# A relational graph layer with a gate: GpSimd's order written out, and two pieces of TensorE's order moved

## The chip, the cores and the metric

The kernel runs on one core of a Trainium2 chip. A core has five engines, each with an instruction queue of its own: TensorE (PE, the matrix products), VectorE (DVE), ScalarE (ACT), GpSimd (POOL) and SyncE (SP, which here only issues DMA transfers). The metric is the device time of one execution in microseconds. The time of a kernel is the median over its runs.

## The reference

A graph of 1250 nodes with 1024 features each, and 20,000 edges of eight relations:

```
x (1250, 1024) f32;  src, dst (20000,) int32, sorted by dst;  edge_type_8 (20000,) in 0..7
weight (8, 1024, 1024), root (1024, 1024), w_gate (2048, 1024), bias, b_gate (1024,)

h   = maximum(layernorm(x), 0)
u   = h @ root + bias
for r in 0..7:                                    # mean over the edges of relation r into a node
    mask = (edge_type_8 == r)
    sums = segment_sum(h[src] * mask[:, None], dst);  cnt = segment_sum(mask, dst)
    u   += (sums / maximum(cnt, 1)[:, None]) @ weight[r]
z   = concatenate([u, h], 1) @ w_gate + b_gate
out = x + tanh(u) * z + h * (1 - z)
```

## The kernel before

**Products.** Since the mean is linear, the kernel multiplies first and gathers afterwards: y_r = h @ weight[r] for all nodes, then u[node] is a weighted sum of rows of y. With `root` and the two halves of `w_gate` there are 11 products of 1280 x 1024 by 1024 x 1024, taken in the order weight[0..7], root (result `hr_dram`), the lower half of w_gate (for h; result `z_dram`), and last the upper half (for u). The nodes are ten blocks of 128 rows. They are worked in five pairs: blocks i and i+5, in the last product 2i and 2i+1. One pair times one matrix is a Strassen-Winograd product (`product`, L192): seven block products instead of eight, each four f32 matmuls of depth 128 onto 128 x 512. A f32 matmul leaves two records in the trace, so a block product has eight of line L201. Products 1 and 2 go to fresh PSUM banks b and c, 3 adds into b, 4 into c, 5 into b, 6 goes to a third bank, 7 adds into b. Between them ScalarE copies a bank out (L210 after the first, L213 after the second, L216 after the third, L223, L231 later) and VectorE adds others (L219, L224, L228). A product that adds into a bank waits for the copy of the bank's last state. The operands on the left (A11, A12, S1 to S4 of `h_op[i]`) come from transposes on TensorE (`transposed`, L177, copied out by ScalarE and VectorE) and four subtractions (`left`, L186 to L190). Those on the right, T1 to T4 (L157, L161, L165, L169), are made by VectorE once for each matrix.

**What sets the order.** `manual_schedule` names the engines that issue in the order of the program's text: PE, DVE, Activation and SP. GpSimd isn't among them: the scheduler chooses its order. After each block product `product` calls `between(j)`, j = 0 to 6; I call these seven places slots. All work beside the products is dealt out there, written as generators that are advanced one `yield` in a slot, so that a `yield` more puts what follows one slot later. In the first products `index()` runs there: `norms()` (layer norm, transposes and operands of pairs 1 to 4) side by side with `columns()`, then `slots()` and `order()`, which sort the edges into a table of slots per node. Pairs 0 and 1 are normed ahead of everything (`both(*b0)`, `both(*b1)`), and pair 1's transposes come in slot 4 of the first product. `both` gives VectorE the statistics and ScalarE the square root and the ReLU (L400, one 128 x 1024 instruction for a block). `with_x` (VectorE) makes x + h, which SP stores as `xh_dram`; `load_x` on SP brings later blocks of x, into buffers of which there are three.

**Edges.** Relations 0 to 2, 3 to 5 and 6 to 7 form three groups. In a group the nodes stand sorted by their count. `rows_and_weights(g)` writes that order to DRAM (ten scatters, L334), loads it back (`node`, L343), makes `node_key` (L344) and gathers the table rows (`idx`, L298), all by GpSimd. `edges(g)` then takes block by block: GpSimd gathers one row of y for each node (L823, into one of four buffers `got`), and VectorE adds it, weighted, to `u` (L829 for the first of group 0, L831 otherwise). A finished block of u is scattered to `u_dram` (`to_rows`, L303), from which the next group gathers it again (L298). Group 0's edges stand beside matrices 4 and 5, group 1's beside 6 and 7, group 2's beside 8 and 9. Group 0's carries along the preparation of groups 1 and 2 (`with_others`: one step of it after every second gather). `spread` deals the steps of a generator evenly over the slots. Ahead of group 1's edges `passes_needed` checks whether any node has more edges than slots: 28 reductions (L897, `far_k`), two small transposes of `most` on TensorE (L901, L902), and a count `n_pass` that all engines read, for a branch that this data doesn't take.

**Gate.** In the last product each pair needs rows that GpSimd gathers in node order: z and xh (`gate_rows`, L1049), hr, added to u by VectorE (`gate_load`, L1024, and behind it the transposes and operands of `gate_u`), and h. `finish` (L1122, L1123) joins them, and GpSimd scatters the rows of `out` (L303). In the text z and xh of a pair stand ahead of hr of the pair two on.

**Dependencies.** The scatters into one buffer write different rows. `declare_no_dep` with a group name tells the framework that they need not wait for each other.

Of the kernel before, what the change touches and what calls it, by code (L numbers as in the profile page):

```python
# [19 lines left out]
def tile_rgcn_highway(  # L20
# [29 lines left out]

    nc = tc.nc
    eng = mybir.EngineType
    ctx.enter_context(tc.manual_schedule(engines={eng.PE, eng.DVE, eng.Activation, eng.SP}))
    P = 128
    N, D = x.shape
    R = weight.shape[0]
# [21 lines left out]

    A11, A12, A22, S1, S2, S3, S4 = range(7)
    A21 = S3  # L80

    def nrows(d):
        return min(P, N - d * P)
# [207 lines left out]
    ids = const.tile([P, ND], I32, name="ids")  # L291
    pos_i = const.tile([P, G, ND], I32, name="pos_i")
    n_pass = const.tile([1, 1], I32, name="n_pass")
    h_op = [keep.tile([P, 7, KQ, P], F32, name=f"h_op{i}") for i in range(NP)]

    def rows_of(to, of, at):
# [3 lines left out]
            in_offset=bass.IndirectOffsetOnAxis(ap=at, axis=0))  # L300

    def to_rows(of, frm, at, group):
        ins = nc.gpsimd.indirect_dma_start(  # L303
            out=of, out_offset=bass.IndirectOffsetOnAxis(ap=at, axis=0), in_=frm, in_offset=None)
        tc.declare_no_dep(ins.ins, group=group, reason="rows differ")
        tc.add_to_no_dep_group(group, ins.ins)

    def slot_rows(g, of, to):
# [22 lines left out]
    def rows_and_weights(g):  # L331

        for d in range(ND):
            ins = nc.gpsimd.indirect_dma_start(  # L334
                out=node_dram[g][:, :],
                out_offset=bass.IndirectOffsetOnAxis(ap=pos_i[:, g, d:d + 1], axis=0),
                in_=ids[:, d:d + 1], in_offset=None,
                bounds_check=KEYS - 1, oob_is_err=False)
            tc.declare_no_dep(ins.ins, group="nodes", reason="places differ")
            tc.add_to_no_dep_group("nodes", ins.ins)  # L340
            if d % 2:
                yield
        nc.gpsimd.dma_start(node[:, g, :], node_dram[g].rearrange("(d p) o -> p (d o)", p=P))  # L343
        nc.gpsimd.tensor_single_scalar(node_key[:, g, :], node[:, g, :], g * KEYS, op=OP.add)  # L344
        yield
        yield
        for d in range(ND):
            rows_of(idx[:, g, d, :], table_rows, node_key[:, g, d:d + 1])
            if d % 2:
                yield  # L350

    with ExitStack() as early:
# [111 lines left out]
        fac[0].make_t3()  # L464
        left(h_op[0], 3)
        b1 = [Normed(1 + part * NP, x1[part], scratch(NP - 1 - part, 2)) for part in range(2)]
        both(*b1)
        fac[0].make_t4()
        for b in b0 + b1:
            b.store()  # L470
        for b in b0:
            b.with_x()
        xs += [load_x(2, 1), load_x(3, 0)]


        tb_col = ix1.tile([P, NCH], F32, name="tb_col")
# [74 lines left out]
        def slots(ix):  # L551
# [78 lines left out]
            def place(j):  # L630
                cs, o = chunks(j), now.pop(j)
                m, c0 = len(cs), cs[0]
                c1 = c0 + m
                p = psum.tile([P, 512], F32, name="ps_q", bufs=1)
                for i in range(m):
                    nc.tensor.matmul(p[:, i * 2 * NHI:(i + 1) * 2 * NHI], o["to_lo"][:, i, :],
                                     o["s_b"][:, i].rearrange("p a b -> p (a b)"),
                                     start=True, stop=True)
                q = p[:, :CG * 2 * NHI].rearrange("p (c a b) -> p c a b", a=2, b=NHI)
                own = ix.tile([P, CG, 2, NHI], F32, name="own", bufs=1)  # L640
                nc.vector.tensor_tensor(
                    own[:, :m], q[:, :m],
                    o["is_at"][:, :m, None, :NHI].to_broadcast([P, m, 2, NHI]), op=OP.mult)
                o2 = ix.tile([P, CG], F32, name="o2")
                nc.vector.reduce_sum(o2[:, :m], own[:, :m].rearrange("p c a b -> p c (a b)"),
                                     axis=AX.X)

                for i, c in enumerate(cs):
                    junk = ix.tile([P, P], F32, name="junk", bufs=1)
                    nc.vector.scalar_tensor_tensor(junk, o["k_bc"][:, i, :], key_col[:, c:c + 1],  # L650
                                                   before, op0=OP.is_equal, op1=OP.mult,
                                                   accum_out=rank[:, c:c + 1])
                nc.vector.tensor_add(rank[:, c0:c1], rank[:, c0:c1], o2[:, :m])
                over = ix.tile([P, CG], F32, name="over")
                nc.vector.tensor_single_scalar(over[:, :m], rank[:, c0:c1], float(SLOTS),
                                               op=OP.is_ge)
                at = ix.tile([P, CG], F32, name="at")
                nc.vector.tensor_add(at[:, :m], first[:, c0:c1], rank[:, c0:c1])
                at_i = ix.tile([P, CG], I32, name="at_i")
                nc.vector.scalar_tensor_tensor(at_i[:, :m], over[:, :m], float(FAR), at[:, :m],  # L660
                                               op0=OP.mult, op1=OP.add)
                for i, c in enumerate(cs):
                    n = nedges(c)
                    ins = nc.gpsimd.indirect_dma_start(  # L664
                        out=table[:, :],
                        out_offset=bass.IndirectOffsetOnAxis(ap=at_i[:n, i:i + 1], axis=0),
                        in_=row_col[:n, c:c + 1], in_offset=None,
                        bounds_check=G * KEYS * WIDE - 1, oob_is_err=False)
                    tc.declare_no_dep(ins.ins, group="scatter", reason="each edge has its own slot")
                    tc.add_to_no_dep_group("scatter", ins.ins)  # L670

            for j in range(ng + 3):
# [8 lines left out]
        def order():  # L681

            with tc.tile_pool(name="sort", bufs=1) as sp:
# [18 lines left out]
                for g in range(G):  # L702
                    ins = nc.sync.dma_start(
                        table[g * KEYS * WIDE:(g + 1) * KEYS * WIDE]
                        .rearrange("(d p s) o -> p d (s o)", p=P, s=WIDE)[:, :, SLOTS:],
                        rc.bitcast(I32))
                    tc.declare_no_dep(ins.ins, group="scatter", reason="beside the slots")
                one = sp.tile([P, 1], F32, name="one")
                nc.vector.memset(one, 1.0)
                for _ in range(4):  # L710
# [22 lines left out]
                    yield  # L733

        def norms():
            for _ in range(4):
                yield
            factored(1, b1)
            left(h_op[1])
            yield  # L740
            for b in b1:
                b.with_x()
            yield
            for i in range(2, NP):
                blocks = []
                if i < NP - 1:
                    blocks = [Normed(i + part * NP, xs.pop(0), scratch(NP - 1, part))
                              for part in range(2)]
                    both(*blocks)
                    yield  # L750
                    for b in blocks:
                        b.store()
                    yield
                    factored(i, blocks)
                    left(h_op[i])
                    yield
                    for b in blocks:
                        b.with_x()
                    xs.append(load_x(i + 1, 1))
                    if i + 2 < NP:  # L760
                        xs.append(load_x(i + 2, 0))
                    yield
                else:
                    for part in range(2):
                        xt = xs.pop(0)
                        b = Normed(i + part * NP, xt, xpool.tile([P, D], F32, name="xt"))
                        b.stats(0)
                        b.stats(1)
                        b.spread()
                        b.scale()  # L770
                        b.relu()
                        b.store()
                        yield
                        transposed(h_op[i], part, b.ht, b.n)
                        b.with_x()
                        yield
                    left(h_op[i])
            first_part.close()
# [19 lines left out]
    with ExitStack() as edges_part:  # L798
# [91 lines left out]
        def passes_needed():  # L890
# [3 lines left out]
            for g in range(G):  # L894
                for d in range(ND):
                    if K[g][d] < SLOTS:
                        nc.vector.reduce_max(far_k[:, g * ND + d:g * ND + d + 1],  # L897
                                             w_of[:, g, d, K[g][d]:], axis=AX.X)
            nc.vector.reduce_max(most[:, 1:2], far_k, axis=AX.X)
            p = bank()  # L900
            nc.tensor.transpose(p[:1, :P], most[:, 0:1], ident)  # L901
            nc.tensor.transpose(p[:1, P:2 * P], most[:, 1:2], ident)  # L902
# [32 lines left out]
        def with_others(e):  # L935
# [6 lines left out]
            for _ in others:  # L942
# [2 lines left out]
        weights(0)  # L945
        s, i = beside(with_others(edges(0, range(ND), u_back(0))), sum(K[0]) + 1, s, i,
                      R0[2] - 1)
        for g in range(1, G - 1):
            if g == G - 2:
                passes_needed()  # L950
            s, i = beside(edges(g, range(ND), u_back(g)), sum(K[g]) + 1, s, i, R0[g + 2] - 1)


        passes = nc.values_load(n_pass[0:1, 0:1], min_val=0, max_val=E // MORE,
# [216 lines left out]
```

## Time and profile before

| | |
|---|---|
| time, median of 3 runs | 1405.44 us (1404.57 to 1406.19) |
| profiled execution: its own time | 1409.36 us |
| its span, first to last instruction | 1407.5 us |
| its granted TensorE clock, mean | 0.991 of full |
| GpSimd's software DMA queue | 48,864 packets, 128.60 MB, 28.3% of the 16 DMA engines |
| SP's and ACT's hardware queues | 101.38 MB, 24.7%; 41.95 MB, 9.1% |
| HBM | 214.20 MB read, 80.65 MB written, 209 GB/s over the span |

The page cuts the span into 40 equal slices; each digit is a busy share, or the granted clock, in tenths:

```profile
PE   5999999999999999899999999999999999999996
...
PEclk8999999999999999999999999999999999999998
```

A row of the timeline has the start in us from the span's start, the length, the engine (a `q` behind it means its queue of DMA issues), the line in the kernel, the operation, output `<-` inputs with shapes, and how many instructions the row joins. In brackets stands how long the engine was idle before it, and what it waited for. A row of the waits has the waiting engine, its tile and line, the releasing engine with tile and line, then total us, how often, and the longest. "DMA node<-node_dram" names a transfer by its destination and source.

### The profile page before, as it was taken

The numbers are of one execution on the slowest core, as the hardware profiler recorded it, in microseconds if no ns is written. First come the engines' busy times: TensorE is split into PE (matmuls) and PEld (weight loads), VectorE is DVE, ScalarE is ACT, GpSimd is POOL, SyncE is SP. The second block draws the span as 40 slices with busy tenths as digits, with TensorE's granted clock in tenths as the row PEclk, the third lists the DMA queues.
The fourth block names the chain that finished last, engine by engine and source line by source line (L and its number), as shares of the span: only waits on it lengthen the run. The fifth ranks groups of instructions, "written<-read, shape, count | busy, mean of one in ns | idle before, by whom it ended". The sixth has DMA issues, their size and how long they took to land.

```text
span 1407.5 us, 11960 instructions
## 1 busy us (share of the span) xinstructions
PE 1369.5 (97%) x3562; PEld 617.6 (44%) x3562; DVE 862.2 (61%) x1658; ACT 339.0 (24%) x721; POOL 624.3 (44%) x537
## 2 busy tenths in 40 slices
PE   5999999999999999899999999999999999999996
PEld 2544444444444444344444444444444444444442
DVE  6764976886768723277454654645445564467983
ACT  3235656566521111011111011111111111122210
POOL 0001655565552657675344443445435433325531
PEclk8999999999999999999999999999999999999998
DMA  8554765775545234458776745888768654557751
GB/s 319 221 185 120 146 156 135 154 160 138 100 109 176 64 107 148 129 203 301 273 252 208 282 146 173 297 300 281 240 241 313 228 163 161 179 187 254 269 174 57
DMA packets 109863, 272.73 MB, mean 194 GB/s; under 512 B 25890, under 2 KB 27920, under 8 KB 109664
## 3 DMA queue, kind: packets, MB, share of 16 engines
q0 software_dynamic: 48864, 128.60, 28.3%
q1 hardware_dynamic: 39808, 101.38, 24.7%
q10 hardware_dynamic: 21120, 41.95, 9.1%
q8 instruction: 28, 0.46, 0.2%
q14 instruction: 43, 0.35, 0.1%
HBM read 214.20 MB, written 80.65 MB: 209 GB/s over the span
## 4 chain that ended last, share of the span: by engine, by line
PE 52%; issue 3%; DVE 2%; DMA 1%; POOL 1%; POOLq 0%; ACT 0%; DVEq 0%; ACTq 0%
PE ps L201 51%; DMA got<-y,idx 0%; PE ps L177 0%; DMA y<-row 0%; POOL out_dram L303 0%; DVE row L1122 0%; DVE u L831 0%; DVE w L1060 0%; DVE u L1024 0%; DVE w L1077 0%; DVE w L165 0%; DVE far_k L897 0%; DVE row L1123 0%; POOL got L298 0%; DVE row L228 0%
## 5 line engine op out<-in xcount | busy, mean ns | idle before, releaser
L201 PE MATMUL ps<-w,h_op 128*128 128x512 f32 x3080 | 1348.6, 597 | 14.3 <-ACT row L210 8.5
L201 PEld LDWEIGHTS ps<-w,h_op 128*128 128x128 f32 x3080 | 581.0, 191 | 711.9 <-issue 692.2
L823 POOL DMA_INDIRECT got<-y,idx x202 | 254.2, 1258 | 272.7 <-DVE u L831 215.6
L831 DVE SCALAR_TENSOR_TENSOR u<-got,w_of,u 128x1024 f32<-128x1024 f32 (+1 forms) x192 | 245.9, 1282 | 138.5 <-DMA got<-y,idx 135.9
L664 POOL DMA_INDIRECT table<-row_col,at_i x157 | 175.7, 1119 | 159.8 <-DVE at_i L660 71.0
L219 DVE TENSOR_TENSOR row<-row,ps 128x512 f32<-128x512 f32 x55 | 37.8, 686 | 158.9 <-PE ps L201 112.4
L223 ACT COPY part<-ps 128x512 f32<-128x512 f32 x55 | 32.1, 585 | 273.3 <-PE ps L201 273.3
L231 ACT COPY row<-ps 128x512 f32<-128x512 f32 x50 | 29.2, 585 | 258.8 <-PE ps L201 253.1
L224 DVE TENSOR_TENSOR row<-row,part 128x512 f32<-128x512 f32 x55 | 38.0, 690 | 61.4 <-ACT part L223 61.3
L210 ACT COPY row<-ps 128x512 f32<-128x512 f32 x55 | 32.1, 583 | 175.6 <-PE ps L201 162.1
L216 ACT COPY row<-ps 128x512 f32<-128x512 f32 x55 | 32.1, 583 | 139.9 <-PE ps L201 139.9
L213 ACT COPY row<-ps 128x512 f32<-128x512 f32 x55 | 32.1, 583 | 130.5 <-PE ps L201 124.6
L650 DVE SCALAR_TENSOR_TENSOR junk<-k_bc,key_col,before 128x128 f32<-128x128 int32 x157 | 55.0, 350 | 4.2
L334 POOL DMA_INDIRECT node_dram<-ids,pos_i x30 | 36.5, 1215 | 39.1 <-issue 38.8
L590 DVE TENSOR_TENSOR seen<-seen,ps_n 128x110 f32<-128x110 f32 x157 | 42.2, 269 | 15.5 <-PE ps_n L585 11.5
L228 DVE TENSOR_TENSOR row<-row,ps 128x512 f32<-128x512 f32 x55 | 37.6, 683 | 21.1 <-PE ps L201 21.1
L567 ACT ACTIVATE is_lo<-io,less_lo 128x128 bf16<-128x128 f32 x157 | 50.1, 391 | 0.8 <-DVE row L224 0.8
L157 DVE TENSOR_TENSOR w<-w,w 128x2048 f32<-128x2048 f32 x11 | 25.2, 2291 | 40.4 <-PE ps L201 39.9
L303 POOL DMA_INDIRECT u_dram<-u,node x20 | 25.2, 1261 | 54.4 <-DVE u L831 40.4
L718 DVE SCALAR_TENSOR_TENSOR junk<-v_bc,val,one 128x1280 bf16<-128x1280 f32 x30 | 46.5, 1550 | 4.0 <-DMA v_bc<-val_dram 3.3
L298 POOL DMA_INDIRECT idx<-table,node_key x30 | 35.8, 1195 | 9.2 <-issue 6.1
L298 POOL DMA_INDIRECT u<-u_dram,node x20 | 20.3, 1015 | 39.4 <-DMA last_dram<-u 14.3
(158 smaller groups left out, 715.3 us busy)
## 6 DMA issues: line engine op xcount, KB each, us to landing
y<-row SPq DMA_DIRECT2D x72, 512.0 KB
w<-in_L_gnn_weight_dram ACTq DMA_DIRECT2D x28, 1024.0 KB
k_bc<-keys_dram SPq DMA_DIRECT2D x39, 256.0 KB
l_bc<-los_dram SPq DMA_DIRECT2D x39, 256.0 KB
w<-in_L_gnn_w_gate_dram ACTq DMA_DIRECT2D x8, 1024.0 KB
hr_dram<-row SPq DMA_DIRECT2D x9, 512.0 KB
z_dram<-row SPq DMA_DIRECT2D x9, 512.0 KB
w<-in_L_gnn_weight_dram SPq DMA_DIRECT2D x4, 1024.0 KB
```

The costliest lines, as they stand in the source:

```text
L201: nc.tensor.matmul(b, aop[:, i, k, :], w.of[i][:, k, :], start=(fresh and k == 0), stop=(k == KQ - 1), skip_group_check=True)
L219: nc.vector.tensor_add(c12, c12, c)
L224: nc.vector.tensor_add(c22, c22, d)
L228: nc.vector.tensor_add(c11, c11, a)
L298: nc.gpsimd.indirect_dma_start(out=to, out_offset=None, in_=of, in_offset=bass.IndirectOffsetOnAxis(ap=at, axis=0))
L567: nc.scalar.activation(is_lo[:, i, :], io, AF.Abs, bias=less_lo[:, c0 + i:c0 + i + 1])
L590: nc.vector.tensor_add(seen[j][:, i, :], was, p[:, i, :])
L650: nc.vector.scalar_tensor_tensor(junk, o["k_bc"][:, i, :], key_col[:, c:c + 1], before, op0=OP.is_equal, op1=OP.mult, accum_out=rank[:, c: ...
L664: ins = nc.gpsimd.indirect_dma_start(out=table[:, :], out_offset=bass.IndirectOffsetOnAxis(ap=at_i[:n, i:i + 1], axis=0), in_=row_col[:n, ...
L718: nc.vector.scalar_tensor_tensor(junk, v_bc[:, g, :], val[:, c:c + 1], one.to_broadcast([P, KEYS]), op0=OP.is_gt, op1=OP.mult, accum_out=p ...
L823: nc.gpsimd.indirect_dma_start(out=t[:n], out_offset=None, in_=y[g][:, :], in_offset=bass.IndirectOffsetOnAxis(ap=at[:n, d, k:k + 1], axis=0),
L831: nc.vector.scalar_tensor_tensor(u[:n], t[:n], w, u[:n], op0=OP.mult, op1=OP.add)
```

## The change

1. GpSimd (`Pool`) joins the engines that issue in the order of the text. The tile `apart` is new: GpSimd clears it (128 x 1) ahead of every scatter of `to_rows`. `declare_no_dep` gets the argument `query=no_wait`, ANY_SYNC, in all four places: the scatters of `to_rows`, of `node_dram` and of the edges into the table, and the store beside the slots.
2. The second pair's norm: `both(*b1)`, `make_t4()` and the stores of h leave the text ahead of the first product, for slot 2, behind its third block product. Pair 1's transposes keep slot 4. `with_x` of pair 0, and the loads of x for the third pair's second block and the fourth pair's first, go to slot 5, `with_x` of pair 1 to slot 6, and one more `yield` puts all later pairs' norms two slots later.
3. `passes_needed` becomes a generator with three `yield`s between the reductions and the transposes. It is advanced once with each step of group 1's edges (`with_passes`).

```diff
-    ctx.enter_context(tc.manual_schedule(engines={eng.PE, eng.DVE, eng.Activation, eng.SP}))
+    ctx.enter_context(tc.manual_schedule(
+        engines={eng.PE, eng.DVE, eng.Activation, eng.Pool, eng.SP}))
...
+    no_wait = mybir.DependencyQuery.ANY_SYNC
...
+    apart = const.tile([P, 1], F32, name="apart")
...
     def to_rows(of, frm, at, group):
+        nc.gpsimd.memset(apart, 0.0)
         ins = nc.gpsimd.indirect_dma_start(
             out=of, out_offset=bass.IndirectOffsetOnAxis(ap=at, axis=0), in_=frm, in_offset=None)
-        tc.declare_no_dep(ins.ins, group=group, reason="rows differ")
+        tc.declare_no_dep(ins.ins, query=no_wait, group=group, reason="rows differ")
...
         b1 = [Normed(1 + part * NP, x1[part], scratch(NP - 1 - part, 2)) for part in range(2)]
-        both(*b1)
-        fac[0].make_t4()
-        for b in b0 + b1:
+        for b in b0:
             b.store()
-        for b in b0:
-            b.with_x()
-        xs += [load_x(2, 1), load_x(3, 0)]
...
         def norms():
-            for _ in range(4):
-                yield
+            yield
+            yield
+            both(*b1)
+            fac[0].make_t4()
+            for b in b1:
+                b.store()
+            yield
+            yield
             factored(1, b1)
             left(h_op[1])
             yield
+            for b in b0:
+                b.with_x()
+            xs.extend([load_x(2, 1), load_x(3, 0)])
+            yield
             for b in b1:
                 b.with_x()
+            yield
             yield
...
             nc.vector.reduce_max(most[:, 1:2], far_k, axis=AX.X)
+            for _ in range(3):
+                yield
             p = bank()
             nc.tensor.transpose(p[:1, :P], most[:, 0:1], ident)
...
+        def with_passes(e):
+            passes = passes_needed()
+            for _ in e:
+                next(passes, None)
+                yield
+
         for g in range(1, G - 1):
-            if g == G - 2:
-                passes_needed()
-            s, i = beside(edges(g, range(ND), u_back(g)), sum(K[g]) + 1, s, i, R0[g + 2] - 1)
+            e = edges(g, range(ND), u_back(g))
+            s, i = beside(with_passes(e) if g == G - 2 else e, sum(K[g]) + 1, s, i, R0[g + 2] - 1)
```

More of the change, by code (lines that the diff above doesn't have):

```diff
@@ L338, in rows_and_weights @@
                 bounds_check=KEYS - 1, oob_is_err=False)
-            tc.declare_no_dep(ins.ins, group="nodes", reason="places differ")
+            tc.declare_no_dep(ins.ins, query=no_wait, group="nodes", reason="places differ")
             tc.add_to_no_dep_group("nodes", ins.ins)
@@ L668, in place @@
                         bounds_check=G * KEYS * WIDE - 1, oob_is_err=False)
-                    tc.declare_no_dep(ins.ins, group="scatter", reason="each edge has its own slot")
+                    tc.declare_no_dep(ins.ins, query=no_wait, group="scatter", reason="each edge has its own slot")
                     tc.add_to_no_dep_group("scatter", ins.ins)
@@ L706, in order @@
                         rc.bitcast(I32))
-                    tc.declare_no_dep(ins.ins, group="scatter", reason="beside the slots")
+                    tc.declare_no_dep(ins.ins, query=no_wait, group="scatter", reason="beside the slots")
                 one = sp.tile([P, 1], F32, name="one")
```

## Prediction

> **What bounds the kernel now.** I read the busy shares first, then the waits of TensorE, then the timeline around each wait, since every product of the text stands in one TensorE queue.
>
> ```profile
> PE 1369.5 (97%) x3562; PEld 617.6 (44%) x3562; DVE 862.2 (61%) x1658; ACT 339.0 (24%) x721; POOL 624.3 (44%) x537
> ...
> PE ps L201 <- ACT row L210: 8.5, 2, 8.2
> ...
> PE ps L177 <- ACT h_op L400: 7.8, 2, 7.6
> ...
> PE ps L201 <- DVE row L228: 5.8, 1, 5.8
> ...
> PE ps L902 <- DVE most L899: 2.1, 1, 2.1
> ```
>
> TensorE bounds it: 97% busy, and what it waits for is a short list (columns: total, times, longest). In quiet stretches 56 L201 records take 24.05 us (the chain of work), so one record is 0.429 us; a block product has eight, so a slot is 3.43 us. The time can only move by what stands around these records: the start (7.6), three waits (8.2, 5.8, 2.1), the slow matmuls after each, new waits, and the tail. The waits answer to the change's parts. The windows of L201 alone show what follows a wait (columns: stretch; length, busy and records; granted clock; DMA share; GB/s):
>
> ```profile
> 27.32:40.72 13.40, 13.40 (x24) 0.77 0.93 339
> 559.78:584.40 24.62, 24.62 (x58) 1.00 0.12 16
> ```
>
> After the first wait 24 records took 13.40 us where 24 x 0.429 = 10.30 would do: 3.1 us more, at a clock of 0.77. After the second, 8 records took 5.17 for 3.43: 1.7 more. After the third, 35 took 16.88 for 15.03: 1.85 more.
>
> **Part 1, the second pair's norm behind the third product.**
>
> ```profile
> 25.56 1.24 ACT L400 ACTIVATE h_op<-h_op,less,rs 128x1024 f32<-128x1024 f32 x1 [0.42 <-DVE less L393]
> 26.71 0.56 ACT L210 COPY row<-ps 128x512 f32<-128x512 f32 x1
> ...
> 27.32 13.56 PE L201 MATMUL ps<-w,h_op 128*128 128x512 f32 x24 [8.16 <-ACT row L210]
> ```
>
> Products 1 and 2 end at 19.16. Product 3 adds into product 1's bank and waits for ScalarE's copy L210, which stands behind the norm of pair 1 (the last L400 ends at 26.80). In the new order L210, L213 and L216 stand ahead of that norm, so product 3 starts at 19.2: its factor T2 is made by 18.0 (L161 from 15.73, 2.28), its operand S2 by 15.8 (L187). Saved: 8.16 + 3.1 = 11.3 us. What is late next: the transposes of pair 1, in TensorE's queue behind product 5, now at 29.4. The norm starts after L216 (23.2) instead of at 22.9, so its last L400 ends near 27.3: 2 us in hand. VectorE's order there is unchanged but for `with_x` and the loads behind it. Those go from 27.6 to about 35.5 (two adds of 1.2), so the SP queue asks for x(2,1) near 39.6 (a store 2.85 later than the add, as 28.89 to 31.74 now); I estimate arrival at 44 to 45.6, 4 to 6 us for 0.5 MB at the 339 GB/s of that stretch. Pair 2's norm starts at slot 8 (45 to 46), takes 5.5 (49.08 to 54.54 now), and its transposes come at 51.9: 0 to 1.3 us in hand, and L216 of that product behind the norm. I take 0.5 us lost, between 0 and 3. Index work starts two slots later and has over 30 us in hand: group 0's last idx gather is issued at 490.03, and weights(0) runs at 530.16.
>
> **Part 2, GpSimd in the order of the text, group 0's gathers.**
>
> ```profile
> 536.02 1.03 POOL L334 DMA_INDIRECT node_dram<-ids,pos_i  x1 [0.30 <-issue]
> ...
> 564.71 1.02 POOL L343 DMA_DIRECT2D node<-node_dram  x1 [5.28 <-DMA node_dram<-ids,pos_i]
> ...
> 581.52 1.02 POOL L823 DMA_INDIRECT got<-y,idx  x1 [0.30 <-issue]
> ...
> 585.93 1.28 DVE L831 SCALAR_TENSOR_TENSOR u<-got,w_of,u 128x1024 f32<-128x1024 f32 x1 [30.62 <-DMA got<-y,idx]
> ```
>
> Now groups 1 and 2's node scatters, loads and idx gathers stand ahead of the fifth row gather; VectorE waits 30.6 us for it with TensorE's row adds queued behind, and TensorE 5.77. The built order puts group 0's gathers right after its own idx gathers (about 497, as two slots later) and deals the other groups out two DMAs per two gathers. So the wait goes: 5.77 + 1.7 + 0.34 (the next L210) = 7.8 us. In its place: group 1's `node` load holds GpSimd for 5.3 (scatters landing) + 2.4 to 6.8 (the load) at most, with up to four gathers out, four slots or 13.7 us of VectorE's work; and VectorE may be some 25 us late (30.6 less 5.8) before TensorE notices. I cost it at nothing; uncovered it would be those 5.8 again. A u scatter now stands behind two row gathers of the next block instead of three: also within that cover. The 30 small memsets `apart` are 0.1 us each (the 128x1 memsets at the start), on an engine busy 44%.
>
> **Part 3, the transposes three slots on.** The first step of edges(1) gathers, and VectorE's order becomes: T4, one L831, far_k's 28 reductions, three L831.
>
> ```profile
> 781.09 2.18 DVE L897 TENSOR_REDUCE far_k<-w_of 128x1 f32<-128x10 f32 x28
> ...
> 793.79 1.28 DVE L831 SCALAR_TENSOR_TENSOR u<-got,w_of,u 128x1024 f32<-128x1024 f32 x1 [6.54 <-DMA got<-y,idx]
> ```
>
> That L831 is group 1's first: it waits for u_dram's last scatter (781.32), the u gather (786.82) and the row gather (788.44), and cannot come sooner. So the reductions end at 793.79 + 1.28 + 2.2 + 0.2 = 797.5. And 76 steps over 70 slots put two steps into slot 0, so "three on" is slot 2: TensorE reaches the transposes after three products, 781.2 + 10.3 = 791.5. It waits 6.0 us where it waited 2.1. With 1.8 for the clock on both sides: 3.9 us lost (bounds 2 and 5.2, the latter with 3.1 for the clock).
>
> **Part 4, GpSimd in order at the gate.** Built order now: xh, xh, hr, hr, z, z. After: z, xh, z, xh, hr, hr.
>
> ```profile
> 1278.84 0.95 POOL L298 DMA_INDIRECT got<-hr_dram,node  x1 [0.30 <-DMA z_dram<-row]
> ...
> 1274.41 1.47 SPq L274 DMA_DIRECT2D z_dram<-row  x2
> ...
> 1286.38 1.23 DVE L1024 TENSOR_TENSOR u<-u,got 128x1024 f32<-128x1024 f32 x1 [8.66 <-DMA got<-hr_dram,node]
> 1288.78 1.23 DVE L1024 TENSOR_TENSOR u<-u,got 128x1024 f32<-128x1024 f32 x1 [1.18 <-DMA got<-hr_dram,node]
> ...
> 1291.91 0.69 DVE L186 TENSOR_TENSOR h_op<-h_op 128x512 f32<-128x512 f32 x1
> ```
>
> The first z gather waits for the last z store, issued by 1275.9 and landed near 1280.6 (a y store took 4.80 in the chain). Behind it stand xh, z, xh, each 1.25 apart, then hr at 1285.7 instead of 1278.84: 6.9 us later. VectorE's L1024 waits for hr, and behind it in its queue L186, ending at 1292.6, which becomes 1299.5. TensorE needs it after product 1 of the next pair, 1297.15 (ScalarE's L210 there starts at 1297.19). Wait: 2.4 us, plus 1.8 of clock = 4.2. The pair after has 3.5 us in hand (L186 done at 1319.4, needed at 1322.95) and a lag of 6.9 - 4.2 = 2.7: no wait. Bounds: 0 (the later hr stays inside the 4.5 us in hand: 1297.15 less 1292.6) and 10 (VectorE has 25.5 of 26 us busy from 1294 to 1320, so a lag is not worked off). After 1359 VectorE is idle again, so the tail keeps.
>
> **Two rules against rows.** (a) After the 2.1 us wait at 783.55 the clock fell (1.85 us). The Trainium skill, "TensorE: Matmul & The Clock Gate", What's actually happening, halves the clock only after an idle window of about 3.4 us: the gate's 2.4 would then cost 2.4, not 4.2. The row decides. (b) The hr gather at 1278.84 was used 7.5 us later. "DMA: Bandwidth & Descriptors", Anatomy of one DMA, fits 2.0 us + bytes/436e3, 3.2 us for these 512 KB: by an estimate from it the second hr (issued 1287.0 to 1287.9) is in at 1291.1, a lag of 2.4, inside the 4.5 in hand, and part 4 is free. I take the row, with the queue it includes, and keep 0 as the end.
>
> **Sum.** -11.3 + 0.5 - 7.8 + 3.9 + 4.2 = -10.5 us. The profiled execution took 1409.36, its span 1407.5 with 1.86 around it: the new span is 1397.0. The median is 3.9 below the profiled time: 1405.4 - 10.5 = 1394.9. With rule (a) alone 1393.1, with (b) 1390.7.
>
> **Rivals.** (R1) The gate absorbs the later hr: 1390.7. For it: the 4.5 us in hand; against: six gathers in a row. (R2) The lag shows again: 3 us in the second gate pair and 2 to 3 at pair 2's transposes: 1399 to 1402. For it: VectorE's full stretch. (R3) Slower: the gate's in-order queue. Without part 4 the change gives 14.7, so it is slower than noise from a gate cost of 17.5 up, which needs a lag of 4.5 + 15.7 = 20 us, hr issued at 1299 instead of 1285.7; three turns in which h, out and z gathers each hold the next hr by another 6.9 would do it. Against: hr of later pairs is issued 10 us before its use (1300.79, 1313.0). Price about 1410. (R4) It does nothing: the early wait comes back whole at the transposes of pairs 1 and 2, and parts 2 and 4 cancel: 1405.
>
> **How the numbers follow.** A measurement here tells 0.2%, 2.8 us, from nothing. Chances: the forecast 0.55 (its own range 1391 to 1399), R1 0.20, R2 0.12, R3 0.08, R4 0.05. Faster is the forecast, R1 and three quarters of R2: 0.84. Same is the rest of R2 and R4: 0.08. Slower is R3: 0.08. The range 1388.5 to 1402.5 leaves out R3, R4 and a little at the low end; its ends are parts 1 to 3 with nothing lost at pair 2 or the gate and part 3 at its lower bound (1388.3), and R2.
>
> **What would show it.** Right: no L201 wait on L210 near 19 us; no VectorE wait over 15 us near 530 to 590; a wait of about 6 us of the second `most` transpose; a z gather ahead of hr and a wait of about 2 us before the second product after it. Wrong: a TensorE wait at pair 1's or 2's transposes above 3 us, a wait on row adds in edges(0) or edges(1), or out scatters later against TensorE's end than now.

## The result: no change that counts, where 10 us were forecast

The changed kernel takes 1408.42 us (median of 17 runs, 1403.71 to 1410.70), the kernel before 1406.23 us (17 runs beside it): ratio 1.0017, 95% interval 1.0006 to 1.0028. That lies outside the forecast range (1388.5 to 1402.5), within 0.2% of the time before.

The profiled execution of the changed kernel took 1409.14 us, its span is 1407.3. TensorE's waits in it (columns: total, times, longest):

```profile
PE ps L915 <- DVE most L910: 14.4, 1, 14.4
PE ps L180 <- ACT h_op L405: 10.9, 3, 7.6
PE ps L204 <- DVE h_op L189: 2.9, 2, 2.8
PE ps L180 <- ACT xt L405: 2.2, 2, 1.4
```

Two of the old waits, 8.2 and 5.8 us, are gone. The one at the small transposes grew from 2.1 to 14.4, and three are new or longer (7.6 of L405 is the start, as before).

**A ledger of TensorE's lead.** ScalarE copies `part` (L223 before, L226 after) behind the fifth block product of each of the 55 pairs. The start of the n-th such copy, less its start in the trace of before, says how far TensorE is ahead (negative) or behind at that place. Where the difference jumps, time was won or lost. For the changed kernel:

| place | lead, us | step | forecast |
|---|---|---|---|
| first pair of the first matrix | -11.7 | first wait gone: -11.7 | -11.3 |
| first pair of the second matrix | -5.5 | other pairs' norms: +6.1 | +0.5 |
| matrix 4, pair 1, then pair 2 | -5.6, -13.7 | group 0's gathers: -8.1 | -7.8 |
| matrix 6, first pair | -1.0 | small transposes: +12.7 | +3.9 |
| last matrix, first pair, then second | -1.0, +5.5 | gate: +6.5 | +4.2 |
| behind the last scatter | -0.2 | end of program: -5.7 | 0 |

So the two profiled executions differ by 0.2 us. The medians differ by 2.2 the other way, because the profiled execution of before is 3.1 us over its own median, that of after 0.7. One term that varies is the old wait in group 0's edges: 5.8 us in that trace, between 0.9 and 6.1 in traces of kernels below that leave GpSimd's order and TensorE's start alone.

**Where the early gain went back.** Timeline of the changed kernel, the fourth pair (index 3):

```profile
64.39 1.57 SPq L369 DMA_DIRECT2D xt<-in_x_dram  x2
...
68.57 0.69 DVE L388 BATCH_NORM_STATS2 st<-xt 128x6 f32<-128x512 f32 x1 [3.75 <-DMA xt<-in_x_dram]
...
69.60 1.24 ACT L405 ACTIVATE h_op<-xt,less,rs 128x1024 f32<-128x1024 f32 x1 [4.39 <-DVE less L398]
...
70.90 1.09 PE L180 MATMUL ps<-ident,h_op 128*128 128x128 f32 x8 [2.50 <-ACT h_op L405]
```

Its second x block gets a buffer only when pair 2's `with_x` is stored. It is loaded at 64.4, and VectorE, ScalarE and TensorE wait for it in turn: 2.50 us and 0.81 at pair 3, 0.79 and 1.45 at pair 4, 5.6 in all, where TensorE had waited 1.1 before. Behind the first of these waits the granted clock was 0.72 over 6 us, which cost about 1.7 more: 6.1 together. In norm_only below the same text waits 4.4 us, the clock stays at 1.00, and 3.3 us go. Pair 2, the one that I had checked, waits for nothing.

**At the small transposes.** The changed kernel, the end of group 0's edges and the start of group 1's:

```profile
764.35 1.03 POOL L308 DMA_INDIRECT u_dram<-u,node  x1 [6.81 <-DVE u L842]
765.69 2.07 POOL L834 DMA_INDIRECT got<-y,idx  x1 [0.31 <-issue]
...
773.63 2.76 POOL L308 DMA_INDIRECT u_dram<-u,node  x1 [5.74 <-DVE u L842]
...
788.63 1.28 DVE L842 SCALAR_TENSOR_TENSOR u<-got,w_of,u 128x1024 f32<-128x1024 f32 x1 [13.10 <-DMA got<-y,idx]
...
792.44 0.37 PE L915 MATMUL ps<-ident,most 128*1 128x128 f32 x1 [14.43 <-DVE most L910]
```

The same place in the kernel before:

```profile
768.00 1.90 POOL L823 DMA_INDIRECT got<-y,idx  x1 [6.67 <-DVE u L831]
770.72 1.04 POOL L303 DMA_INDIRECT u_dram<-u,node  x1 [0.81 <-issue]
...
781.32 0.96 POOL L303 DMA_INDIRECT u_dram<-u,node  x1 [9.57 <-DVE far_k L893]
```

TensorE is 13.7 us earlier here. Group 0's last scatter is only 7.7 earlier (773.63 against 781.32), and the first row add of group 1 only 5.2 (788.63 against 793.79), and the reductions stand behind it. Before, the scheduler let the last gather of rows (768.00) pass the scatter (770.72). In the order of the text it stands behind it, and these two scatters first wait 6.8 and 5.7 us for VectorE.

The edges are not late because TensorE is early. I count from TensorE's own place, the last copy of `part` in matrix 5. In all five traces with GpSimd's order left to the scheduler, group 0's last scatter comes 6.8 us behind that copy, whether TensorE is 6.3 us early there (end_copy) or 3.7 late (norm_only). With the order of the text it comes 12.9 us behind it in the change, and 14.5 to 16.7 in the six other kernels that keep the scatters' place, at leads of 9.4 to 20.9 us. So the edges move with TensorE, and the order makes them 6 to 10 us later. Of the 8.4 us of waiting beyond the forecast's 6.0, 6.1 are this delay. The other 2.4 lie between that scatter and group 1's first row add (15.0 us, against 12.6 in passes_only): its row gather took 7.7 us from issue to use, 5.4 before. Why it took longer is open.

**At the gate.** The changed kernel; the window's columns are stretch; length, busy and records; granted clock; DMA share; GB/s:

```profile
1279.75 0.95 POOL L302 DMA_INDIRECT h_op<-z_dram,node  x1 [17.39 <-issue]
...
1284.75 0.94 POOL L302 DMA_INDIRECT got<-hr_dram,node  x1 [0.30 <-issue]
...
1293.85 2.46 DVE L1042 TENSOR_TENSOR u<-u,got 128x1024 f32<-128x1024 f32 x2 [17.10 <-DMA got<-hr_dram,node]
...
1298.96 13.63 PE L204 MATMUL ps<-w,h_op 128*128 128x512 f32 x24 [2.77 <-DVE h_op L189]
```

```profile
1298.96:1303.00 4.04, 4.04 (x5) 0.50 0.86 302
1303.00:1307.00 4.00, 4.00 (x8) 0.73 0.40 127
```

hr was issued at 1284.75 (forecast 1285.7), TensorE waited 2.8 us (forecast 2.4). Behind it 24 records took 13.63 us for 10.30: 3.3 us of lower clock where I had charged 1.8. The transposes of the next pair took 0.4 more, since a weight load among them waited for VectorE (L1140).

That last wait is the larger part elsewhere. In pool_only, with the same order at the gate, the clock stayed at 1.00 over the 8 us behind the wait:

```profile
1298.02 10.57 PE L204 MATMUL ps<-w,h_op 128*128 128x512 f32 x24 [2.71 <-DVE h_op L189]
...
1312.92 0.66 PE L180 MATMUL ps<-ident,u 128*128 128x128 f32 x4 [3.02 <-DVE row L1127]
```

Counted from the first wait, TensorE got to those transposes 3 us earlier and waited 3.0 us there for VectorE's `finish` (L1127, L1140 in the change). Five more traces with this order have that second wait, of 1.4 to 3.2 us. The forecast said "no wait" of the later hr's second appearance; in the trace of the change the slow matmuls only hid it.

### The profile page after: what moved, and what is told of

Same layout as the page of the kernel before. It is cut to its first block, busy times and chain, and to the rows that moved or that the text cites. A ratio compares the mean times of both kernels' runs of the same rounds, so it can differ in the third digit from the quotient of the medians.

```text
span 1407.3 us, 11968 instructions
## 1 busy us (share of the span) xinstructions
PE 1369.7 (97%) x3562; PEld 617.4 (44%) x3562; DVE 862.4 (61%) x1658; ACT 339.4 (24%) x721; POOL 616.8 (44%) x567
## 4 chain that ended last, share of the span: by engine, by line
PE 72%; issue 9%; DMA 6%; POOL 5%; DVE 2%; ACT 0%; POOLq 0%; DVEq 0%; ACTq 0%
PE ps L204 71%; DMA got<-y,idx 3%; DMA node_dram<-ids,pos_i 2%; POOL got L834 2%; POOL got L302 1%; POOL out_dram L308 1%; DMA got<-hr_dram,node 1%; PE ps_n L585 1%; DVE u L842 1%; DMA got<-h_dram,node 1%; POOL u_dram L308 1%; PE ps L180 0%; POOL idx L302 0%; POOL h_op L302 0%; DMA xh_dram<-xt 0%
## 5 line engine op out<-in xcount | busy, mean ns | idle before, releaser
L834 POOL DMA_INDIRECT got<-y,idx x202 | 244.8, 1212 | 243.1 <-DVE u L842 163.4
L664 POOL DMA_INDIRECT table<-row_col,at_i x157 | 179.3, 1142 | 159.1 <-DVE at_i L660 65.7
L226 ACT COPY part<-ps 128x512 f32<-128x512 f32 x55 | 32.2, 586 | 291.2 <-PE ps L204 282.6
L308 POOL DMA_INDIRECT u_dram<-u,node x20 | 29.6, 1480 | 76.6 <-DVE u L842 72.8
```

Source lines behind the costliest of these rows:

```text
L308: ins = nc.gpsimd.indirect_dma_start(out=of, out_offset=bass.IndirectOffsetOnAxis(ap=at, axis=0), in_=frm, in_offset=None)
L664: ins = nc.gpsimd.indirect_dma_start(out=table[:, :], out_offset=bass.IndirectOffsetOnAxis(ap=at_i[:n, i:i + 1], axis=0), in_=row_col[:n, ...
L834: nc.gpsimd.indirect_dma_start(out=t[:n], out_offset=None, in_=y[g][:, :], in_offset=bass.IndirectOffsetOnAxis(ap=at[:n, d, k:k + 1], axis=0),
```

## The experiments

Each ratio is against runs of the kernel before beside it (medians 1406.24 us for passes_only, pool_only, norm_only and reduce_first; 1404.17 for scatter_later, hr_first, norms_later and end_copy; 1406.44 for passes_back and all_four). The ledger, in us against the trace of before, for all kernels whose TensorE work is told of below:

| kernel | matrix 1 | before group 0's wait | behind it | behind the small transposes | before the gate | end |
|---|---|---|---|---|---|---|
| the change | -5.5 | -5.6 | -13.7 | -1.0 | -1.0 | +5.5 |
| norm_only | -8.4 | -8.4 | +3.7 | +1.9 | +1.9 | +1.9 |
| pool_only | -1.4 | -1.3 | -9.4 | -1.8 | -1.8 | +6.1 |
| passes_only | -0.2 | -0.7 | +0.7 | +4.3 | +4.3 | +4.3 |
| passes_back | -8.2 | -8.3 | -16.4 | -7.8 | -7.8 | -1.6 |
| scatter_later | -7.2 | -7.3 | -15.4 | -11.5 | -11.6 | -3.7 |
| reduce_first | -8.7 | -8.7 | -16.8 | -21.0 | -20.8 | -16.0 |
| hr_first | -8.5 | -8.5 | -16.6 | -1.9 | -1.9 | -1.9 |
| norms_later | -14.6 | -12.8 | -20.9 | -6.2 | -6.2 | -0.1 |
| all_four | -14.3 | -13.6 | -21.7 | -25.9 | -25.6 | -25.1 |

### One part alone: passes_only, pool_only, norm_only

The kernel before with one of the three parts of the change, as the diff above has it: `with_passes` and three yields; Pool in the list with `no_wait` and `apart`; the moved norm.

> The kernel before with the third change alone: the small transposes three steps on. Theory: the reductions stand behind the first row add of group 1, which comes when it came before (about 794 us), and TensorE is there at 791.5: a wait of 6 us instead of 2, +3.9 us against before. It is the TensorE that comes earlier in the whole change that makes 14 of 6. Rival: the place costs by itself what the whole change showed, a wait of 12 to 14 us, +12 us.

> The kernel before with the first change alone: GpSimd in the order of the text, with the cleared tile and the argument of the no-dependency calls. Theory: -8.1 us in group 0's edges, +6.5 at the gate, so -1.6 us against before, and the small transposes wait about as before (2 us). Rival (the forecast's terms): -7.8 + 4.2 = -3.6 us. Other rival: the order alone makes the edges' tail so late that the wait at the small transposes grows by itself, to 6 us or more, and the kernel is slower than before by 2 us or more.

> The kernel before with the second change alone: the second pair's norm and its company in the text's new places, later pairs' norms two slots later; GpSimd and the transposes as before. Theory (ledger of the two traces): the first wait goes, 11.7 us, and 6.1 come back as waits of TensorE at the transposes of pairs 2 and 3 (counting from 0: the third and fourth norms to come), whose x arrives late: -5.5 us against before, waits of L177's successor on L405 of some 5 us between 65 and 100 us. Rival (the forecast's own term): -10.8 us, no wait above 1.5 us there.

Measured: passes_only 1413.08 us, ratio 1.0049 (1.0035 to 1.0062); pool_only 1408.23, 1.0020 (1.0010 to 1.0029); norm_only 1410.55, 1.0030 (1.0019 to 1.0041). (In the last expectation the pairs meant are those with index 3 and 4.) Each part alone makes the kernel slower. The lines on the small transposes in the waits of TensorE, first passes_only, then pool_only:

```profile
PE ps L904 <- DVE most L899: 6.0, 1, 6.0
```

```profile
PE ps L907 <- DVE most L904: 9.9, 1, 9.9
```

In passes_only the wait is the forecast's 6.0 us and the step in the ledger +3.6: the arithmetic of that part was right with the edges in the scheduler's order. That an earlier TensorE makes 14 of these 6 us, as the expectation adds, did not hold: the next two sections show what does. (The median is 6.8 us over before, the ledger ends at +4.3, since its trace of before is itself 3.1 us over the median.) In pool_only the transposes have not moved, and the wait is 9.9: my second rival. GpSimd's order by itself makes the end of group 0's edges late. norm_only, waits of TensorE and GpSimd's timeline:

```profile
PE ps L201 <- DVE row L228: 17.3, 1, 17.3
```

```profile
567.74 1.02 POOL L343 DMA_DIRECT2D node<-node_dram  x1 [5.16 <-DMA node_dram<-ids,pos_i]
...
584.47 1.02 POOL L829 DMA_INDIRECT got<-y,idx  x1 [0.30 <-issue]
```

TensorE arrives 8.4 us earlier at group 0's wait, and the fifth row gather comes 3.0 us later than before (584.47 against 581.52), as the index work does. The wait grows from 5.8 to 17.3: everything that the norm gives is spent there. So -11.7 and -8.1 are not two gains side by side; the first is kept only with the second. My theory for this run, -5.5 us, was wrong in just this.

### Undoing the third part: passes_back

```diff
-            for _ in range(3):
-                yield
...
-            s, i = beside(with_passes(e) if g == G - 2 else e, sum(K[g]) + 1, s, i, R0[g + 2] - 1)
+            if g == G - 2:
+                passes_needed()
+            s, i = beside(edges(g, range(ND), u_back(g)), sum(K[g]) + 1, s, i, R0[g + 2] - 1)
```

> The changed kernel with its third part undone: the reductions and the small transposes stand where they stood before, ahead of group 1's edges; the norm and GpSimd's order stay changed. Theory: it isn't the three slots that cost 14 us but that TensorE comes earlier while the last row adds of group 0 do not: the reductions, ready at about 776.5 us in the trace with reductions first, meet a TensorE that reaches the transposes at 764 to 767 us. A wait of 10 to 13 us stays at the second small transpose, and the time is within 3 us of the changed kernel (1 to 3 under). Rival: the place does it; the wait is 2 to 4 us and the kernel 10 us or more under the changed one.

Measured: 1402.11 us, ratio 0.9964 (0.9953 to 0.9975).

```profile
PE ps L913 <- DVE most L910: 10.0, 1, 10.0
```

The wait that stays, 10.0 us, has the size that the theory says, but not its cause. In pool_only, with the transposes in the same place, TensorE is 7.0 us later (-9.4 against -16.4 behind group 0's wait), and the wait is the same 9.9. It is GpSimd's order that makes it, not TensorE's lead. The time is 0.5% under the change, some 7 us, more than the 1 to 3 that I expected: the step at the transposes is +8.6 instead of +12.7, and the rest is the smaller loss in the first matrix in this execution. The third part made a bad place worse; it did not make it bad.

### Scatters behind more gathers: scatter_later

```diff
-                    if k == min(1, last):
-                        leave()
-                        if d != blocks[-1]:
-                            ahead = new_u(d + 1, of, g)
+                    if k == min(1, last) and d != blocks[-1]:
+                        ahead = new_u(d + 1, of, g)
+                    if k == min(3 if g < G - 1 else 1, last):
+                        leave()
```

> The changed kernel, but in groups 0 and 1 the scatter of a finished block of u stands behind the fourth row gather of the next block instead of behind the second (blocks with fewer slots: behind their last). Theory: of the 14.4 us of waiting at the second small transpose, 6 are the forecast's, and about 6 come from the tail of group 0, where each scatter waits for VectorE's last add of its block and holds the next block's gathers behind it, so that the last block is that much later against TensorE than before. With the scatters later the wait is 7 to 9 us and the kernel 5 to 7 us under the changed one. Rival: the tail is late because gathers themselves are slow there; the wait stays 13 to 15 us, the time within 2 us of the changed kernel.

Measured: 1402.02 us, ratio 0.9987 (0.9973 to 1.0000), against 1.0017 for the change.

```profile
PE ps L915 <- DVE most L910: 6.3, 1, 6.3
```

From 14.4 to 6.3 by the place of GpSimd's scatters alone, with the transposes where the change has them and TensorE 1.7 us further ahead. Group 0's last scatter is back at 7.0 us behind TensorE's place. What is left is the forecast's 6.0. The step in the ledger falls from 12.7 to 3.9. By the ratios the kernel is some 4 us under the change, less than the 5 to 7 expected: the gate took 7.8 us instead of 6.5.

### Reductions ahead of the edges: reduce_first

```diff
-            for _ in range(3):
+            for _ in range(12):
                 yield
...
             passes = passes_needed()
+            next(passes, None)
             for _ in e:
```

> The changed kernel, but the 28 reductions stand ahead of the first gather of group 1 instead of behind its first row add, and the transposes twelve steps on instead of three. Theory: the wait of 14.4 us at the second small transpose and the 1.8 us of lower clock after it go, nothing takes their place: 16 us faster than the changed kernel, about 14 us under before. Rival: VectorE is late with the row adds anyway, since its first one of group 1 waits for its gather 15 us past the slot, and TensorE waits 5 to 14 us at the next product that adds into a bank: no better than 2 to 10 us under the changed kernel.

Measured: 1389.72 us, ratio 0.9890 (0.9874 to 0.9906). The wait is gone and no other takes its place: the ledger goes from -16.8 to -21.0 at the transposes, 4.2 us better than before, and stays there to the gate. VectorE's late row adds disturb nobody but the transposes. This one step was worth the difference between nothing and 16 us.

### hr first: hr_first

```diff
+                if i + 2 < NP and j == 0:
+                    gate_load(i + 2, j)
                 gate_rows(i, j)
                 if j == 1:
                     scatter_outs()
-                if i + 2 < NP:
+                if i + 2 < NP and j > 0:
                     gate_load(i + 2, j)
```

> The changed kernel, but in the last product the gathers of hr stand ahead of the gathers of z and xh in the text. Theory: the wait of VectorE for hr (17 us) and with it TensorE's 2.8 us and the slow matmuls behind it go: 6.5 us faster than the changed kernel in the last product, about 4 us under before. Rival: z and xh come too late instead and VectorE is late with the end of the first pair: no gain, within 2 us of the changed kernel.

Measured: 1402.59 us, ratio 0.9991 (0.9981 to 1.0002). VectorE's second add of hr starts at 1283.1, not at 1295.1 (the second of the two at 1293.85 above):

```profile
1283.08 1.23 DVE L1042 TENSOR_TENSOR u<-u,got 128x1024 f32<-128x1024 f32 x1 [1.19 <-DMA got<-hr_dram,node]
```

The gate's step is 0.0 instead of +6.5. z and xh, later now, keep TensorE waiting nowhere. By the ratios the kernel is some 4 us under the change, less than the 6.5 expected.

### Later norms: norms_later

```diff
                 blocks = []
+                if i == 3:
+                    yield
+                    yield
...
                         b.store()
                         yield
+                        yield
                         transposed(h_op[i], part, b.ht, b.n)
```

> The changed kernel, but pair 3's norm (the fourth) stands two more slots later, and each half of the last pair's transposes one more slot behind its norm. Theory: TensorE's waits at these transposes (5.6 us by the trace, and the slow matmuls behind the first) go: 3 to 6 us faster than the changed kernel by the ledger of the first matrix; but what TensorE gains there is spent again at the wait of the second small transpose, which the edges of group 0 set, so the time moves by less than 2.5 us and that wait grows by 3 to 6 us. Rival: the gain comes through, 3 to 6 us under the changed kernel.

Measured: 1404.82 us, ratio 0.9997 (0.9983 to 1.0012). The waits at pairs 3 and 4 are gone, and the lead after the first matrix is 14.6 us instead of 5.5. Behind the small transposes it is 6.2 instead of 1.0:

```profile
PE ps L919 <- DVE most L914: 15.6, 1, 15.6
```

Of 9 us won some 4 were lost there and before, and by the ratios about 0.2%, 2 to 3 us, came through: between the theory and its rival. The theory's reason fell. The wait grew by 1.2 us, not by 3 to 6, and in hr_first, with a TensorE 4.3 us later, it is the same 15.6.

### The end of the program: end_copy, query_only, copy_between

The drain of GpSimd at the end of the kernel before and of the changed one (columns: ns shortest/median/longest, first and last start):

```profile
L1167 POOLq DRAIN  x3: 46/112/10191, 1396.4 to 1407.2; - x3
```

```profile
L1185 POOLq DRAIN  x3: 46/112/4453, 1401.9 to 1407.1; - x3
```

5.7 us, which I had not expected at all. Three kernels ask what goes with it: a copy on GpSimd ahead of each scatter of `out`, in the kernel before; the argument `query=no_wait` alone, in all its four places, in the kernel before; and, in the changed kernel, a copy in place of the clearing of `apart`.

```diff
+                nc.gpsimd.tensor_copy(apart[:n], t[:n, 0:1])
                 to_rows(out, t[:n], node[:n, LG, d:d + 1], "out")
```

```diff
-        tc.declare_no_dep(ins.ins, group=group, reason="rows differ")
+        tc.declare_no_dep(ins.ins, query=no_wait, group=group, reason="rows differ")
```

```diff
-        nc.gpsimd.memset(apart, 0.0)
+        nc.gpsimd.tensor_copy(apart, eps)
```

> The kernel before with one addition: ahead of each scatter of rows of the output GpSimd copies one column of these rows into a small tile, so that an instruction of its own stands between the last scatters. Theory: in the three kernels with GpSimd's order by the scheduler 9.9 us pass between the end of the last scatter's issue and the end, in the three with the cleared tile between scatters 4.2; it is the instruction between them that makes GpSimd's drain short: 5.7 us under before. Rival: it has to do with GpSimd's order or the dependency argument; the time stays that of before, within 1.5 us.

> The kernel before with the new argument of the no-dependency calls alone; the order of instructions on GpSimd is that of before. Question: what shortens GpSimd's drain at the end from 10.2 to 4.5 us. If the argument does it, the drain is 4.5 us here; if it is GpSimd's order or the cleared tile, it is 10.2. The time is that of before but for that.

> The changed kernel, but GpSimd copies one column into the tile ahead of each scatter instead of clearing it. GpSimd's order is that of the changed kernel. Question: is it the clearing or the order that goes with a drain of 4.5 us at the end instead of 10.2. If the clearing, the drain is 10.2 us here and the time 5.7 us over the changed kernel; if the order, 4.5 us and the time of the changed kernel.

end_copy: 1403.93 us, ratio 1.0002 (0.9991 to 1.0012), drain 10.2 us; my theory fell. query_only: a single run, 1407.60, drain 10.2. copy_between: a single run, 1415.11, drain 4.5.

The short drain goes with GpSimd's order, whether a clearing or a copy stands between the scatters: 4.4 to 4.5 us in all traces with Pool in the list, 10.2 in all without. All kernels with Pool in the list also have the argument and an instruction ahead of each scatter, so the order without these two was not tried. Why the drain is shorter stays open. copy_between's run is long since the wait at the small transposes was 20.5 us in it; whether the copies or that execution made it so was not tried.

### Together: all_four

The edits of reduce_first, hr_first, norms_later and scatter_later in the changed kernel.

> The changed kernel with all four edits: reductions ahead of group 1's first gather and transposes twelve steps on, hr ahead of z and xh, the later norms later, u scatters behind the fourth gather. Theory: the terms add up where no later wait takes them: 16.5 under before for the first, 4.8 for hr, 1 to 5 for the norms, nothing for the scatters since no one waits for them any more: 22 to 26 us under before. Rival: TensorE, earlier still, meets VectorE's late row adds in the edges, and no more than 17 us are left.

Measured: 1378.87 us, ratio 0.9807 (0.9794 to 0.9820): 27 us under the kernel before. In the first matrix nothing is given back any more, at the gate 0.6 us, and TensorE's waits are the start and 0.6 us besides.

## Why the prediction was wrong

- **Part 1, the wait removed** ("11.3 us"): right, 11.7. **"What is late next"** failed. I followed the later norms to pair 2 and took 0.5 us, between 0 and 3; pair 2 waits for nothing, pairs 3 and 4 wait 5.6, and with the clock 6.1 us went (3.3 to 5.8 in the other traces with the same text there). The chain that I left out is the x buffers: three of them, each freed by a `with_x` of the pair before. The rows of pair 3 show it, and in norms_later, which gives pair 3's load two more slots and the last pair's one, the waits are gone.
- **Part 2, group 0's gathers** ("7.8 us"): right, 8.1 in every trace with GpSimd in order. That a u scatter behind two gathers instead of three is "also within that cover", and so costs nothing, is the step that decided. In the last blocks, with three or four slots, each scatter holds the next gathers back until VectorE is through. The edges end 6 us later against TensorE, and more in the other traces. pool_only has that delay as a wait of 9.9 us for 2.1, at the old place of the transposes; scatter_later takes it away, 14.4 us to 6.3.
- **Part 3, the transposes** ("It waits 6.0 us"): exact alone (passes_only), and in the sum 14.4, +12.7 us for +3.9. The term took the edges' end to stand where it stood against TensorE. That TensorE came earlier did not spoil it: in scatter_later it comes earlier still, and the wait is 6.3. The scatters of part 2 spoiled it.
- **Part 4, the gate**: order and first wait right (2.4 forecast, 2.8). That a lag of 2.7 makes "no wait" behind it was wrong, as the second wait in pool_only and five other traces shows: I had checked the next operand (L186), not VectorE's `finish` ahead of the next transposes. Wrong too was the 1.8 us for the clock as a fixed price of a short wait: 3.3 in the change, none in pool_only behind nearly the same wait (clock 1.00). Rule (a), of the Trainium skill, "TensorE: Matmul & The Clock Gate", What's actually happening, charges nothing behind so short a wait: pool_only agrees, and the change, where the clock fell to 0.50, does not. Rule (b), "DMA: Bandwidth & Descriptors", Anatomy of one DMA, gives an estimate of 3.2 us for such a gather; this queue gave 9.1 us from the first hr's issue to its use.
- **The tail** ("keeps"): wrong in the other direction, -5.7 us. That was luck: no term had it, and without it the change would be 5.5 us behind in these two traces.
- Of the rivals, R4 had the time (1405) with another mechanism: I let the early wait come back whole at pairs 1 and 2. R1 did not happen. R2's second wait at the gate is not in the trace of the change, but in six others. R3's price was nearly reached, at the transposes and not at the gate.

In one sentence: the gains were right, and the sum was wrong because two costs were taken as covered that were not, the u scatters (nothing, for some 8 us of waiting at the transposes) and the later norms (0.5 us, for 6.1).

## What to carry to other kernels

A scatter in an in-order queue that waits for a result also holds the gathers behind it. Before calling it covered, follow the queue into the shortest blocks, where few gathers run ahead. Here it helped to put it behind four gathers, as many as there are buffers; other numbers were not tried.

When a change makes the bounding engine earlier, ask at every later wait whether the chain that it waits for moves along. Group 0's edges did, at leads from +3.7 to -21.7 us. The index work ahead of them did not in the scheduler's order, and norm_only lost all its gain there.

A check that nobody needs soon (here the reductions and transposes) belongs ahead of the first step that waits for DMA, with its reader far behind: reduce_first moved both, and 16 us came of it.

## What the runs showed of the hardware

- TensorE's granted clock can fall behind a wait of 2 to 3 us, and need not. The same wait of 2.1 us at the transposes was followed by a mean of 0.66 over 5 us in the kernel before, and by 1.00 in norm_only, query_only and end_copy. At the gate a mean of 0.61 over 8 us followed 2.8 us of waiting in the change, and 1.00 followed 2.7 us in pool_only. Nor did the loss follow the length: 1.85 us behind 2.1, 3.3 behind 2.8, 3.1 behind 8.2.
- GpSimd's drain at the end took 10.2 us in the five kernels with its order left to the scheduler and 4.4 to 4.5 in those with the order of the text, with the last scatters issued alike.
- TensorE's wait in group 0's edges lasted 0.9 us in one execution and 5.3 to 6.1 in three others with the same order of instructions there: a ledger from one execution carries some us of that.
